# The division of a linear attention: two 32x32-square transposes on VectorE in place of TensorE transposes there and back

## The chip, the cores and the metric

The kernel runs on one NeuronCore of a Trainium2 chip. The metric is device time in microseconds (us); lower is better. The core's engines each take their instructions in order: TensorE (PE; its weight loads are listed apart as PEld), VectorE (DVE), ScalarE (ACT), GpSimd (POOL) and SyncE (SP, which here only starts DMAs). Data lies in SBUF, with 128 partitions; TensorE writes to PSUM, which is used here as 8 banks of 128x512 f32.

## What is computed

One decoder layer over x of shape (32, 128, 256), 32 sequences of 128 positions with 256 features. Three residual blocks, each ahead of a layer norm. Cut to what matters here:

```python
def attn(x):                                  # A: causal linear attention, 16 heads of 16
    q, k = phi(x @ Wq.T + bq), phi(x @ Wk.T + bk)      # phi = elu + 1
    v = x @ Wv.T + bv
    num = einsum('bhsd,bhsde->bhse', q, cumsum(k[..., :, None] * v[..., None, :], 2))
    den = einsum('bhsd,bhsd->bhs', q, cumsum(k, 2))
    return (num / (den[..., None] + 1e-6)) @ Wo.T + bo
x = x + attn(layernorm(x))
x = x + softmax_cross_attention(layernorm(x), ctx_1024)   # B: 16 heads, no output projection
x = x + ffn(layernorm(x))                     # 256 -> 1024 gated, two 1024x1024 gelu layers, -> 256
```

## The kernel before

The 32 sequences are handled as 16 pairs. `xs[m]` holds pair m, 128 positions on the partitions. The first stretch of the program does attention A and attention B, the rest the feed-forward network in eight blocks of four sequences.

**A, for pair m and sequence j of it.** `a_norm` takes statistics on VectorE, finds 1/sqrt on GpSimd by three Newton rounds (lines 145 to 149, twelve tiny instructions), and normalizes on GpSimd. `a_transpose` turns the result to features-on-partitions (TensorE, line 349, and a ScalarE copy). `a_keys` and `a_queries` project it (line 359), apply phi (two Exp and two Relu on ScalarE, lines 463 and 465, then one VectorE instruction, line 467), and for the queries GpSimd makes two copies masked by parity of head (`qa2`, line 381). `a_values` adds the bias to v on VectorE (line 480); next to each head's 16 columns of v stand 16 columns of ones. `a_scores` multiplies keys by queries (line 388, tile `sa`, two halves of two banks each) and VectorE multiplies each half by the causal mask (line 494, tile `at`). `a_weighted` multiplies v with ones by these weights: `pf` has, for head 4i+g, on partitions 32g to 32g+31 and in column block i, 16 rows of the numerator and 16 equal rows of the denominator. It ends with a ScalarE copy to SBUF (`fa`, line 412). `a_divide` transposes the four blocks back on TensorE (`po`, line 419), so that positions lie on the partitions, and VectorE adds the epsilon, takes the reciprocal and multiplies (lines 423, 424, 428). `a_turn` transposes the quotient on TensorE once more (two blocks, `pot`, line 512), and ScalarE copies it to SBUF (`oT`, line 514). `a_out` multiplies by Wo (line 367, `pw`) and VectorE adds to x (line 519).

**B** is softmax attention with the same tiling: `b_maxima` (`sm`, and two VectorE maxima, line 565, 1.2 us each), `b_turn_maxima` (`pz`, `mT`), `b_scores` (`se`, Exp on ScalarE, line 598), `b_weighted` and `b_divide`, which share the functions `weighted` and `divided` with A; b_divide's GpSimd addition is line 606.

**Order.** Every engine's order is the order in which the instructions are written, by lists of units: `first` for steps m = 0, 1, 2; `both` for m = 3 to 15, where A of pair m is interleaved with B of pair m - 3; `begins` for m = 16; then lists with B and feed-forward work only. A unit `(f, ahead, j)` stands for f on pair m + ahead (for b_ units m - 3 + ahead); one that was already done is left out. Before step 0 a short opening does keys, values and queries of the first pairs, after twelve transposes of the identity into a tile that nobody reads (`idle`, line 700).

**Buffers that make one unit wait for another.** The score tiles `sm`, `sa` and `se` share the same four PSUM banks (two tags with one buffer each): `sa` can't be written before VectorE has read `sm`, `se` not before VectorE has read `sa`, the next `sm` not before ScalarE has read `se`. All else on TensorE goes through four other banks (tag `m`). `fa`, `oa`, `oT` have two buffers each.

Of the kernel before, what the change touches and what calls it, by code (L numbers as in the profile page):

```python
# [9 lines left out]
F32 = mybir.dt.float32  # L10
# [3 lines left out]
ALU = mybir.AluOpType  # L14
# [3 lines left out]
P = 128  # L18
B, S, D = 32, 128, 256
H, HD = 16, 16  # L20
HID = 1024
DC = D // P
# [7 lines left out]
VW = 2 * HD  # L30
LN_EPS = 1e-5
ATTN_EPS = 1e-6
# [14 lines left out]
def decoder_block_kernel(  # L47
# [14 lines left out]
    nc = tc.nc  # L62
# [4 lines left out]
    small = ctx.enter_context(tc.tile_pool(name="small", bufs=4))  # L67
# [5 lines left out]
    ident = const.tile([P, P], F32, name="ident")  # L73
# [55 lines left out]
    def pair_stats(n, nmean, rstd, engine=nc.gpsimd):  # L129

        mv = small.tile([P, 2, 2], F32, tag="mv", name="mv")
        for j in range(2):
            st = small.tile([P, 6], F32, tag="st", name="st")
            nc.vector.bn_stats(out=st, in_=xs[n][:, j, :])
            nc.vector.bn_aggr(out=mv[:, j, :], in_=st)
        nc.vector.tensor_scalar(nmean, mv[:, :, 0], -1.0, None, ALU.mult)


        v = small.tile([P, 2], F32, tag="v", name="v")
        nc.vector.tensor_scalar(v, mv[:, :, 1], LN_EPS, None, ALU.add)  # L140
        nc.vector.tensor_scalar(rstd.bitcast(I32), v.bitcast(I32), -0.5, RSQRT_SEED, ALU.mult, ALU.add)
        hv = small.tile([P, 2], F32, tag="hv", name="hv")
        nc.vector.tensor_scalar(hv, v, -0.5, None, ALU.mult)  # L143
        t = small.tile([P, 2], F32, tag="t", name="t")
        for _ in range(NEWTON):
            engine.tensor_tensor(t, rstd, rstd, ALU.mult)  # L146
            engine.tensor_tensor(t, t, hv, ALU.mult)
            engine.tensor_scalar(t, t, 1.5, None, ALU.add)
            engine.tensor_tensor(rstd, rstd, t, ALU.mult)
# [112 lines left out]
    with tc.manual_schedule(engines=ORDERED):  # L262
# [7 lines left out]
        def buffer(shape, dtype, tag, name, **kw):  # L270
            side = att_a if tag in A_TAGS else att_b
            return side.tile(shape, dtype, tag=tag, name=name, **kw)
# [55 lines left out]
        def bank(name):  # L328
            return ps_m.tile([P, 4, S], F32, tag="m", name=name)
# [63 lines left out]
                    stop=stop,  # L393
                )

        def weighted(weights, v, tag):

            pf = bank("pf")
            for i in range(4):
                for g in range(G):
                    nc.tensor.matmul(  # L404
                        pf[32 * g : 32 * g + 32, i, :],
                        lhsT=v[:, 4 * i + g, :],
                        rhs=weights[g // 2][:, g % 2, i, :],
                        start=True,
                        stop=True,
                    )  # L410
            f = buffer([P, 4, S], F32, tag=tag, name=tag)
            nc.scalar.copy(f, pf)
            return f

        def divided(f, add, tag):

            po = bank("po")
            for i in range(4):
                nc.tensor.transpose(po[:, i, :], f[:, i, :], ident)  # L419
            po = po.rearrange("p i (g w) -> p (i g) w", w=VW)  # L420
            rden = small.tile([P, H], F32, tag="rden", name="rden", bufs=2)
            if add:
                nc.vector.tensor_scalar(rden, po[:, :, HD], add, None, ALU.add)
                nc.vector.reciprocal(rden, rden)
            else:
                nc.vector.reciprocal(rden, po[:, :, HD])
            o = buffer([P, D], F32, tag=tag, name=tag)
            nc.vector.tensor_tensor(
                o.rearrange("p (h e) -> p h e", e=HD),
                po[:, :, 0:HD],  # L430
                rden.unsqueeze(2).to_broadcast([P, H, HD]),
                ALU.mult,
            )
            return o
# [8 lines left out]
        A = [dict() for _ in range(NPAIR)]  # L443
# [56 lines left out]
                weights.append(at)  # L500

        def a_weighted(m, j):
            A[m]["f", j] = weighted(A[m].pop(("w", j)), A[m]["v"][:, j], "fa")

        def a_divide(m, j):
            A[m]["o", j] = divided(A[m].pop(("f", j)), ATTN_EPS, "oa")

        def a_turn(m, j):
            pt = bank("pot").rearrange("p a s -> p (a s)")[:, : DC * S]
            o = A[m].pop(("o", j))  # L510
            for c in range(DC):
                nc.tensor.transpose(pt[:, ts(c, P)], o[:, ts(c, P)], ident)
            oT = buffer([P, DC, S], F32, tag="oT", name="oT")
            nc.scalar.copy(oT.rearrange("p c s -> p (c s)"), pt)
            A[m]["oT", j] = oT

        def a_out(m, j):
            pp = token_major(bank("pw").rearrange("p a s -> p (a s)")[:, :D], WO, A[m].pop(("oT", j)))
# [3 lines left out]
        Bs = [dict() for _ in range(NPAIR)]  # L522
# [76 lines left out]
                weights.append(pr)  # L599

        def b_weighted(m, j):
            Bs[m]["f", j] = weighted(Bs[m].pop(("w", j)), Bs[m]["v"][:, j], "fb")

        def b_divide(m, j):
            o = divided(Bs[m].pop(("f", j)), None, "ob")
            nc.gpsimd.tensor_tensor(xs[m][:, j, :], xs[m][:, j, :], o, ALU.add)
            if j == 1:
                pair_stats(m, nmean3[:, 2 * m : 2 * m + 2], rstd3[:, 2 * m : 2 * m + 2])
# [3 lines left out]

        both = [
            (b_maxima, 0, 0), (b_weighted, -1, 1), (a_divide, -1, 1), (b_transpose, 1), (b_values, 1),
            (a_scores, 0, 0), (b_turn_maxima, 0, 0), (b_divide, -1, 1), (a_turn, -1, 1), (a_transpose, 1),
            (b_queries, 1), (b_scores, 0, 0), (a_weighted, 0, 0), (a_out, -1, 1), (b_norm, 2), (a_keys, 1),
            (b_maxima, 0, 1), (b_weighted, 0, 0), (a_divide, 0, 0), (a_bias, 1), (a_queries, 1),
            (a_scores, 0, 1), (b_turn_maxima, 0, 1), (b_divide, 0, 0), (a_turn, 0, 0), (b_keys, 1),
            (b_scores, 0, 1), (a_weighted, 0, 1), (a_out, 0, 0), (a_norm, 2), (a_values, 1), (b_load, 2),
        ]  # L620
        first = [
            (a_scores, 0, 0), (a_norm, 2), (a_turn, -1, 1), (a_keys, 1), (a_out, -1, 1), (b_norm, 2),
            (a_weighted, 0, 0), (a_bias, 0), (a_scores, 0, 1), (a_divide, 0, 0), (a_queries, 1),
            (b_transpose, 1), (a_values, 1), (a_weighted, 0, 1), (a_turn, 0, 0), (a_bias, 1),
            (b_queries, 1), (a_transpose, 2), (a_out, 0, 0), (a_divide, 0, 1), (b_load, 2),
        ]
        prologue = SKEW

# [9 lines left out]
        def settle():  # L638
# [6 lines left out]

        begins = [
            (b_load, 2), (b_maxima, 0, 0), (b_weighted, -1, 1), (a_divide, -1, 1), (b_transpose, 1),
            (b_values, 1), (b_turn_maxima, 0, 0), (a_turn, -1, 1), (b_divide, -1, 1), (a_out, -1, 1), beside,
            (b_queries, 1), (b_scores, 0, 0), beside,
            (b_norm, 2), (b_maxima, 0, 1), settle, (b_weighted, 0, 0), beside,  # L650
            (b_turn_maxima, 0, 1), (b_divide, 0, 0), settle, (b_keys, 1), (b_scores, 0, 1), beside,
# [44 lines left out]
            fill(v)  # L696

        idle = bank("idle")
        for n in range(12):
            nc.tensor.transpose(idle[:, n % 4, :], ident, ident)  # L700
        a_norm(0)
        b_keys(0)
# [10 lines left out]
        for m in range(NPAIR + SKEW + 1):  # L713
            waiting = None
            if m >= prologue and spare:
                n = spare.pop(0)
# [101 lines left out]
    with tc.If(n_inexact > 0):  # L818
        with tc.tile_pool(name="wg", bufs=1) as wg, tc.tile_pool(name="hig", bufs=2) as hig, tc.tile_pool(
            name="ps_g", bufs=8, space=PSUM  # L820
# [23 lines left out]
            for b in range(B):  # L844
# [5 lines left out]
                for c in range(DC):  # L850
                    pt = ps_g.tile([P, TB], F32, tag="mm", name="gpt")
# [90 lines left out]
```

## Time and profile before

| | |
|---|---|
| median of 3 runs | 1135.28 us (1133.74 to 1136.63) |
| profiled execution | 1138.04 us, of which span 1136.2 us |
| attention steps 0 to 2 (list `first`) | 18.8 to 66.4 us of the span |
| attention steps 3 to 15 (list `both`) | 66.4 to 408 us |
| one step of `both` | 28.6 us |
| busy in a step of `both` | PE 28.6, DVE 22.4, ACT 14.0, POOL 17.0 us |
| granted TensorE clock, mean | 0.997 |

The span is what the hardware profiler recorded from the first to the last instruction. A timeline line gives start, duration, engine, source line, operation, output<-inputs, shape and count, and in brackets how long the engine had been idle before it and what ended the wait. Consecutive TensorE instructions overlap, so their durations do not add up: what a group costs TensorE is the distance from its start to the start of the next group.

### The profile page before, as it was taken

What the parts mean: (1) busy time and instruction counts of PE and PEld (TensorE: products, weight loads), DVE (VectorE), ACT (ScalarE), POOL (GpSimd) and SP (SyncE); (2) the same over time, 40 slices, a digit from 0 to 9 for tenths busy, and PEclk for the clock granted to TensorE, in tenths of its full rate; (3) what the DMA queues carried; (4) which work ended last, traced back from release to release, by engine and by line L of the source; (5) the groups of instructions that cost most, each with busy time, mean ns of one, the idle gap of its engine ahead of it and who ended that gap; (6) DMA issues with size and microseconds to landing.
All of it is one profiled execution on the core that took longest, in us unless ns stands there. A gap on an engine that the chain in (4) does not pass through costs nothing.

```text
span 1136.2 us, 20345 instructions
## 1 busy us (share of the span) xinstructions
PE 1117.1 (98%) x8238; PEld 902.7 (79%) x8238; DVE 577.3 (51%) x1296; ACT 411.4 (36%) x655; POOL 446.8 (39%) x1025
## 2 busy tenths in 40 slices
PE   8899999999999999999999999999999999999997
PEld 6677777777777777767888888888888888888886
DVE  6667777777777776532243433522522522422411
ACT  4344444444444446861221221321311312312311
POOL 3655555555555546454231321321311312312311
PEclk9999999999999999999999999999999999999999
DMA  8001111111111100005000111000000000000000
GB/s 274 1 20 48 47 48 48 48 48 48 48 48 48 48 11 11 1 1 185 20 26 31 38 38 38 19 14 5 29 5 5 19 1 2 18 1 15 5 1 22
DMA packets 26548, 39.28 MB, mean 35 GB/s; under 512 B 2512, under 2 KB 18640, under 8 KB 26448
## 3 DMA queue, kind: packets, MB, share of 16 engines
q1 hardware_dynamic: 22000, 26.09, 6.8%
q0 software_dynamic: 4032, 11.54, 3.2%
q8 instruction: 67, 1.10, 0.4%
q10 hardware_dynamic: 416, 0.28, 0.1%
q14 instruction: 33, 0.27, 0.1%
HBM read 33.71 MB, written 4.19 MB: 33 GB/s over the span
## 4 chain that ended last, share of the span: by engine, by line
PE 88%; DVE 3%; POOL 3%; ACT 2%; issue 2%; DMA 1%; SPq 0%; POOLq 0%; DVEq 0%; ACTq 0%
PE ph L218 47%; PE pp L359 9%; PE py L762 5%; PE pf L404 5%; PE pv L367 4%; PE se L388 3%; PE sa L388 3%; PE sm L388 3%; PE pw L367 3%; PE po L419 2%; PE pt L349 1%; DMA H<-in_h2T_dram 1%; DVE at L494 1%; PE se L588 1%; DVE nm L565 1%
## 5 line engine op out<-in xcount | busy, mean ns | idle before, releaser
L181 DVE TENSOR_TENSOR gl<-hg,gh 128x512 fp32r<-128x512 f32 x126 | 87.7, 696 | 345.5 <-POOL gh L180 342.6
L180 POOL CAST gh<-hg 128x512 fp32r<-128x512 f32 x128 | 79.1, 618 | 362.0 <-ACT hg L242 362.0
L242 ACT ACTIVATE hg<-ph,col 128x512 f32<-128x512 f32 x128 | 88.3, 690 | 366.8 <-PE ph L218 366.8
L218 PE MATMUL ph<-sl,H 128*128 128x512 f32 x512 | 199.3, 389 | 0.8 <-POOL sl L181 0.8
L218 PE MATMUL ph<-gl,H 128*128 128x512 f32 x512 | 199.4, 389 | 0.4 <-DVE gl L181 0.4
L218 PE MATMUL ph<-sh,H 128*128 128x512 f32 x512 | 199.6, 390 | 0.1
L218 PE MATMUL ph<-gh,H 128*128 128x512 f32 x512 | 199.4, 390 | 0.0
L218 PEld LDWEIGHTS ph<-sl,H 128*128 128x128 f32 x512 | 96.1, 188 | 21.0 <-POOL sl L181 1.2
L218 PEld LDWEIGHTS ph<-gl,H 128*128 128x128 f32 x512 | 96.1, 188 | 21.0 <-DVE gl L181 1.1
L218 PEld LDWEIGHTS ph<-sh,H 128*128 128x128 f32 x512 | 96.1, 188 | 20.9 <-POOL sh L180 0.6
L218 PEld LDWEIGHTS ph<-gh,H 128*128 128x128 f32 x512 | 96.1, 188 | 20.4 <-POOL gh L180 0.6
L218 PE MATMUL ph<-xh,W 128*128 128x512 f32 x256 | 100.6, 393 | 0.0
L218 PE MATMUL ph<-xl,W 128*128 128x512 f32 x256 | 99.8, 390 | 0.0
L180 POOL CAST sh<-hs 128x512 fp32r<-128x512 f32 x64 | 58.5, 915 | 66.8 <-DVE hs L234 66.8
L565 DVE TENSOR_REDUCE nm<-sm 128x8 f32<-128x1024 f32 x64 | 75.2, 1217 | 17.6 <-PE sm L388 17.6
L494 DVE TENSOR_TENSOR at<-sa,causal 128x1024 f32<-128x1024 f32 x64 | 75.2, 1215 | 8.0 <-PE sa L388 8.0
L232 ACT ACTIVATE sil<-ph,col 128x512 f32<-128x512 f32 x64 | 44.1, 689 | 74.9 <-PE ph L218 74.8
L234 DVE SCALAR_TENSOR_TENSOR hs<-ph,col,sil 128x512 f32<-128x512 f32 x64 | 48.0, 750 | 36.2 <-PE ph L218 20.1
L598 ACT ACTIVATE pr<-se 128x1024 f32<-128x1024 f32 x64 | 62.0, 1022 | 11.9 <-PE se L588 11.9
L146 POOL TENSOR_TENSOR t<-rstd 128x2 f32<-128x2 f32 x138 | 32.5, 235 | 83.3 <-DVE hv L143 76.1
L359 PE MATMUL pp<-xTa,WA 128*128 128x256 f32 x256 | 62.2, 388 | 0.7 <-ACT xTa L351 0.7
L762 PE MATMUL py<-W,gh 128*128 128x256 f32 x256 | 62.6, 285 | 0.0
(133 smaller groups left out, 1933.3 us busy)
## 6 DMA issues: line engine op xcount, KB each, us to landing
x<-in_x_dram SPq DMA_DIRECT2D x16, 256.0 KB, 5.7
cT<-in_ctxT_dram SPq DMA_DIRECT2D x16, 256.0 KB, 2.6
stage<-in_h1T_dram SPq DMA_DIRECT2D x16, 256.0 KB, 2.8
H<-in_h1T_dram POOLq DMA_DIRECT2D x8, 512.0 KB, 3.6
H<-in_h2T_dram POOLq DMA_DIRECT2D x8, 512.0 KB, 8.1
out_dram<-y SPq DMA_DIRECT2D x32, 128.0 KB, 1.7
raw<-in_h2T_dram SPq DMA_DIRECT2D x16, 256.0 KB, 2.8
WA<-in_wattn_dram SPq DMA_DIRECT2D x4, 256.0 KB, 4.7
```

What stands on the lines that cost most here:

```text
L180: (high_engine.copy if high_engine is nc.scalar else high_engine.tensor_copy)(high, t)
L181: lows.append(lambda: low_engine.tensor_tensor(low, t, high.bitcast(F32), ALU.subtract))
L218: nc.tensor.matmul(pp, lhsT=w[:, k, ts(c, P)], rhs=parts[p], start=(k == 0 and p == 0), stop=(k == len(src) - 1 and p == 1),)
L242: nc.scalar.activation(t, pp, AF.Gelu, scale=col[:, c_scale + c : c_scale + c + 1])
L359: nc.tensor.matmul(pp[:, c, :], lhsT=w[:, d, ts(c, P)], rhs=src[:, d, :], start=(d == 0), stop=(d == DC - 1))
L367: nc.tensor.matmul(pp, lhsT=src[:, d, :], rhs=w[:, d, :], start=(d == 0), stop=(d == DC - 1))
L388: nc.tensor.matmul(sc[g // 2][:, g % 2, 2 * c : 2 * c + 2, :], lhsT=loaded[32 * g : 32 * g + 32, c, ts(j, S)], rhs=streamed[32 * g : 32 * ...
L404: nc.tensor.matmul(pf[32 * g : 32 * g + 32, i, :], lhsT=v[:, 4 * i + g, :], rhs=weights[g // 2][:, g % 2, i, :], start=True, stop=True,)
L494: nc.vector.tensor_tensor(at.rearrange("p g i s -> p (g i) s"), sc[u].rearrange("p g i s -> p (g i) s"), causal.unsqueeze(1).to_broadcast( ...
L565: nc.vector.tensor_reduce(nm[:, 2 * u : 2 * u + 2, :], sc[u], AX.X, ALU.max, negate=True)
L598: nc.scalar.activation(pr, sc[u], AF.Exp)
L762: nc.tensor.matmul(py[:, :D], lhsT=h[k][p][:, ts(j, S)], rhs=W3[:, k, :], start=(k == 0 and p == 0), stop=(k == HC - 1 and p == 1),)
```

## The change

In A only, the quotient is formed without TensorE. `weighted` returns `pf`, still in PSUM. `block_divided`, called from `a_weighted`, has VectorE transpose each 32x32 square of `pf` on its own, from PSUM to SBUF: partition 32g+w, block i, position s goes to partition 32g + (s mod 32), block i, square s div 32, column w. Numerator and denominator of a head and position then lie on one partition. VectorE adds the epsilon and takes the reciprocal (now from SBUF), and GpSimd multiplies. `features`, called from `a_divide`, transposes the quotient's squares back on VectorE, which gives features on partitions, in the order of heads that the squares leave. The host permutes the columns of Wo to this order. `a_turn` is gone. B keeps the old way.

With it the lists change: `a_turn` is taken out of `both`, `begins` and `first`; in `first` the units `a_divide` and `b_norm` also stand in other places. The opening's unread transposes go from 12 to 20.

```diff
-            f = buffer([P, 4, S], F32, tag=tag, name=tag)
-            nc.scalar.copy(f, pf)
-            return f
+            return pf
+        def block_divided(pf, add, tags):
+            f = buffer([P, 4, S], F32, tag=tags[0], name=tags[0])
+            nc.vector.transpose(f.rearrange("p i s -> p (i s)"), pf.rearrange("p i s -> p (i s)"))
+            f = f.rearrange("p i (b w) -> p b i w", w=VW)
+            rden = small.tile([P, 4, 4], F32, tag="rden", name="rden", bufs=2)
+            if add:
+                nc.vector.tensor_scalar(rden, f[:, :, :, HD], add, None, ALU.add)
+                nc.vector.reciprocal(rden, rden)
+            else:
+                nc.vector.reciprocal(rden, f[:, :, :, HD])
+            o = buffer([P, 4, 4, HD], F32, tag=tags[1], name=tags[1])
+            nc.gpsimd.tensor_tensor(
+                o, f[:, :, :, 0:HD], rden.unsqueeze(3).to_broadcast([P, 4, 4, HD]), ALU.mult
+            )
+            return o
+        def features(o, tag):
+            oT = buffer([P, DC, S], F32, tag=tag, name=tag)
+            nc.vector.transpose(
+                oT.rearrange("p c (b q) -> p b c q", q=32), o.rearrange("p b (c e) d -> p b c (e d)", e=2)
+            )
+            return oT
...
         def a_weighted(m, j):
-            A[m]["f", j] = weighted(A[m].pop(("w", j)), A[m]["v"][:, j], "fa")
+            pf = weighted(A[m].pop(("w", j)), A[m]["v"][:, j])
+            A[m]["o", j] = block_divided(pf, ATTN_EPS, ("fa", "oa"))
         def a_divide(m, j):
-            A[m]["o", j] = divided(A[m].pop(("f", j)), ATTN_EPS, "oa")
-
-        def a_turn(m, j):
-            pt = bank("pot").rearrange("p a s -> p (a s)")[:, : DC * S]
-            o = A[m].pop(("o", j))
-            for c in range(DC):
-                nc.tensor.transpose(pt[:, ts(c, P)], o[:, ts(c, P)], ident)
-            oT = buffer([P, DC, S], F32, tag="oT", name="oT")
-            nc.scalar.copy(oT.rearrange("p c s -> p (c s)"), pt)
-            A[m]["oT", j] = oT
+            A[m]["oT", j] = features(A[m].pop(("o", j)), "oT")
...
         first = [
-            (a_scores, 0, 0), (a_norm, 2), (a_turn, -1, 1), (a_keys, 1), (a_out, -1, 1), (b_norm, 2),
-            (a_weighted, 0, 0), (a_bias, 0), (a_scores, 0, 1), (a_divide, 0, 0), (a_queries, 1),
-            (b_transpose, 1), (a_values, 1), (a_weighted, 0, 1), (a_turn, 0, 0), (a_bias, 1),
-            (b_queries, 1), (a_transpose, 2), (a_out, 0, 0), (a_divide, 0, 1), (b_load, 2),
+            (a_scores, 0, 0), (a_norm, 2), (a_keys, 1), (a_divide, -1, 1), (a_out, -1, 1),
+            (a_weighted, 0, 0), (a_bias, 0), (a_scores, 0, 1), (a_queries, 1), (a_divide, 0, 0),
+            (b_transpose, 1), (a_values, 1), (a_weighted, 0, 1), (a_bias, 1), (b_norm, 2),
+            (b_queries, 1), (a_transpose, 2), (a_out, 0, 0), (b_load, 2),
         ]
...
         idle = bank("idle")
-        for n in range(12):
+        for n in range(20):
             nc.tensor.transpose(idle[:, n % 4, :], ident, ident)
...
-                (a[n][by_group] if n[-2:] in ("Wq", "Wk") else a[n]).T
+                (a[n][by_group] if n[-2:] in ("Wq", "Wk") else a[n][:, by_group] if n[-2:] == "Wo" else a[n]).T
```

More of the change, by code (lines that the diff above doesn't have):

```diff
@@ L394, in scores, with weighted @@
                 )
-        def weighted(weights, v, tag):
+        def weighted(weights, v):
             pf = bank("pf")
@@ L410, in weighted, with divided @@
                     )
-            f = buffer([P, 4, S], F32, tag=tag, name=tag)
-            nc.scalar.copy(f, pf)
-            return f
-        def divided(f, add, tag):
+            return pf
[20 more added lines that the diff above has]
+            return oT
+        def divided(f, tag):
             po = bank("po")
@@ L421, in divided @@
             rden = small.tile([P, H], F32, tag="rden", name="rden", bufs=2)
[L422 to L426, printed above, removed]
+            nc.vector.reciprocal(rden, po[:, :, HD])
             o = buffer([P, D], F32, tag=tag, name=tag)
@@ L601, in b_weighted @@
         def b_weighted(m, j):
-            Bs[m]["f", j] = weighted(Bs[m].pop(("w", j)), Bs[m]["v"][:, j], "fb")
+            pf = weighted(Bs[m].pop(("w", j)), Bs[m]["v"][:, j])
+            Bs[m]["f", j] = f = buffer([P, 4, S], F32, tag="fb", name="fb")
+            nc.scalar.copy(f, pf)
         def b_divide(m, j):
-            o = divided(Bs[m].pop(("f", j)), None, "ob")
+            o = divided(Bs[m].pop(("f", j)), "ob")
             nc.gpsimd.tensor_tensor(xs[m][:, j, :], xs[m][:, j, :], o, ALU.add)
@@ L614, in decoder_block_kernel @@
             (b_maxima, 0, 0), (b_weighted, -1, 1), (a_divide, -1, 1), (b_transpose, 1), (b_values, 1),
-            (a_scores, 0, 0), (b_turn_maxima, 0, 0), (b_divide, -1, 1), (a_turn, -1, 1), (a_transpose, 1),
+            (a_scores, 0, 0), (b_turn_maxima, 0, 0), (b_divide, -1, 1), (a_transpose, 1),
             (b_queries, 1), (b_scores, 0, 0), (a_weighted, 0, 0), (a_out, -1, 1), (b_norm, 2), (a_keys, 1),
             (b_maxima, 0, 1), (b_weighted, 0, 0), (a_divide, 0, 0), (a_bias, 1), (a_queries, 1),
-            (a_scores, 0, 1), (b_turn_maxima, 0, 1), (b_divide, 0, 0), (a_turn, 0, 0), (b_keys, 1),
+            (a_scores, 0, 1), (b_turn_maxima, 0, 1), (b_divide, 0, 0), (b_keys, 1),
             (b_scores, 0, 1), (a_weighted, 0, 1), (a_out, 0, 0), (a_norm, 2), (a_values, 1), (b_load, 2),
@@ L647, in decoder_block_kernel @@
             (b_load, 2), (b_maxima, 0, 0), (b_weighted, -1, 1), (a_divide, -1, 1), (b_transpose, 1),
-            (b_values, 1), (b_turn_maxima, 0, 0), (a_turn, -1, 1), (b_divide, -1, 1), (a_out, -1, 1), beside,
+            (b_values, 1), (b_turn_maxima, 0, 0), (b_divide, -1, 1), (a_out, -1, 1), beside,
             (b_queries, 1), (b_scores, 0, 0), beside,
```

## The prediction

> **What bounds it now.** I read the page's busy line first, then a table by stage, then TensorE's timeline of one step.
>
> ```profile
> PE 1117.1 (98%) x8238; PEld 902.7 (79%) x8238; DVE 577.3 (51%) x1296; ACT 411.4 (36%) x655; POOL 446.8 (39%) x1025
> ```
>
> ```profile
> 179.10:207.70 28.60, 28.58 (x321) 21.81 (x320) 22.37 (x59) 13.96 (x25) 17.04 (x49) 1.00 0.15 48
> ```
>
> In one step of `both` (columns: length; then busy time of PE, PEld, DVE, ACT, POOL; clock) TensorE has no idle time and VectorE is busy 22.4 of 28.6 us. TensorE work that is taken out shortens the step, unless VectorE, which gets work, is late with something TensorE needs. Where it is close to that shows in the timeline of the step from 207.69 to 236.3:
>
> ```profile
> 209.78 0.66 PE L419 MATMUL po<-ident,fa 128*128 128x128 f32 x4
> 210.27 0.60 PE L349 MATMUL pt<-ident,xnb 128*128 128x128 f32 x4
> ...
> 214.21 0.38 PE L512 MATMUL pot<-ident,oa 128*128 128x128 f32 x2
> 214.43 0.60 PE L349 MATMUL pt<-ident,xna 128*128 128x128 f32 x4
> 215.05 1.99 PE L359 MATMUL pp<-xTb,WB 128*128 128x256 f32 x8
> ...
> 226.49 1.50 PE L388 MATMUL sa<-qa,ka 32*128 32x256 f32 x16
> ...
> 230.56 1.57 PE L388 MATMUL se<-qb,kb 32*128 32x256 f32 x14
> ```
>
> Distances between starts: the four `po` transposes cost 0.49 us, the two `pot` 0.22. An undisturbed score group takes 1.15 us on a line of its own; the `sa` with 1.50 and the `se` with 1.57 already wait inside for the VectorE reads that free their banks.
>
> **What is removed.** Per step two times (0.49 + 0.22) = 1.42 us of TensorE. The `pp` after `pot` and `pt` started 0.62 after `pt` instead of 0.43: it waited for the copy that frees `pot`'s bank, so 0.19 more. At most 1.6 us a step. Two ScalarE copies (0.59 and 0.37 us) go too, worth nothing: ScalarE idles half the step.
>
> **What VectorE gets.** No row shows a square transpose. The nearest rows, one pass over the same shapes:
>
> ```profile
> L480 DVE TENSOR_TENSOR va<-pv,row 128x512 f32<-128x512 f32 x14 | 9.6, 684 | 1.3 <-PE pv L367 1.3
> L428 DVE TENSOR_TENSOR oa<-po,rden 128x256 f32<-128x256 f32 x30 | 12.7, 425 | 1.0
> ```
>
> I take 0.68 us for 128x512 and 0.42 for 128x256 (0.60 and 0.35 start to start). Lower end: the same. Upper end: line 494's 1024 columns take 1215 ns, 0.53 us more than 512, so about 1 ns a column; at twice that the two transposes would take 1.2 and 0.7. A rule speaks against the change: the Trainium skill, "VectorE: DVE Perf Modes", The three transpose paths, gives 311 ns for 128x128 bf16 squares on VectorE. If the cost went with the number of calls of 128 columns, 512 would be 1.24; if a fixed part is paid once, 0.71. The row decides for the latter, the former is my upper end. Addition and reciprocal stay (0.17 + 0.25), the 0.42 multiply leaves VectorE. Balance: +0.68 per sequence, 1.4 a step: 23.7 of some 27.2 us.
>
> **Where it lies.** (1) The 128x512 transpose comes behind `pf`, ahead of the x addition. There VectorE now waits:
>
> ```profile
> 206.07 0.42 DVE L519 TENSOR_TENSOR x<-pw,x 128x256 f32<-128x256 f32 x1 [2.31 <-PE pw L367]
> ...
> 220.47 0.42 DVE L519 TENSOR_TENSOR x<-pw,x 128x256 f32<-128x256 f32 x1 [1.14 <-PE pw L367]
> ```
>
> `pf` was done at 204.97; transpose, addition and reciprocal end at 204.97 + 0.6 + 0.2 + 0.3 = 206.1: hidden to within 0.1. Every further 0.1 us of transpose comes out late. What is then late: statistics, v, the weight tests, the maxima (line 565) and so `sa`. (2) The 128x256 transpose (0.35) takes the place of 0.9 us of division between maxima and mask; VectorE gets there 0.5 us sooner.
>
> Walking the step (time from its start; before in brackets): maxima end 4.55 (4.5); TensorE reaches `sa` at 4.35 (4.84) and half of it waits: end 5.6 (5.9). `se` at 8.4 (9.3), its `pot` and the bank wait gone. `pf` 9.7, keys end 13.5 (14.4), then Exp/Relu, line 467 and maxima to 18.2 (19.1). TensorE, without the second `po`, is at the second `sa` at 17.4 and waits to 18.2: this `po`'s 0.49 is half lost here. Masks end 22.05 (23.4), because the short transpose replaced the division; second `se` and `pf` follow 1.3 us sooner. **The step is 27.3 us, 1.3 less.** Twelve such, and 0.9 in step 3: -16.5. Step 16: -0.6.
>
> **GpSimd gets** a multiply of 128x256 with two inputs, like line 606 (0.72 us; the broadcast and the rows of 16 are in no row: 0.5 to 1.5). That is 1.45 a step beside 17.0. In the step it is hidden: the first multiply ends about 16.7 and is wanted at 18.6, the second has over 5 us; only above 2.7 us would it make the short transpose late, and with it the masks. In the opening it isn't hidden.
>
> **The opening, steps 0 to 2.** Here waits set the time:
>
> ```profile
> 48.85 1.15 PE L388 MATMUL sa<-qa,ka 32*128 32x256 f32 x16 [2.79 <-POOL qa L381]
> 49.92 0.44 PE L512 MATMUL pot<-ident,oa 128*128 128x128 f32 x2
> 50.20 3.54 PE L359 MATMUL pp<-xTa,WA 128*128 128x256 f32 x8
> ```
>
> ```profile
> 50.00:60.00 10.00, 10.00 (x82) 0.83 0.00 1
> ```
>
> After 2.8 us of idling the clock fell (0.83 here, i.e. 3.4 us at half): eight matmuls took 3.33 us instead of 1.73, 1.6 lost. In the new list `b_norm` (Newton and normalize, 4.8 us of GpSimd) no longer stands ahead of the queries' masks: that wait goes. But others come. Step 0: GpSimd is the chain (Newton, normalize, bias, masks) and has one multiply more: +0.7. Steps 1 and 2: `a_out` of the pair before stands behind `a_divide`, whose VectorE transpose is queued behind masks, statistics and line 467. `pw` can start some 6.1 and 7.3 us into the step, where TensorE is free at 2.8: idling 3.4 and 4.5 us, then `pf`, the next scores and their masks are late. Step 1 still gets 1.7 shorter, as the masks are sooner; step 2 0.8 longer. Sum of the three: -0.2. Step 3: `b_norm(1)` now comes after the last `a_weighted` of step 2, and `b_transpose(1)` is the second thing TensorE does in step 3. From the end of `pf`: transpose, addition and reciprocal 1.1, then on GpSimd multiply 0.72 and bias 1.4 (the statistics, 1.7, lie beside these), Newton and normalize 4.8: 8.0 us; TensorE has 1.7 + 0.4 + 0.9 + 1.1 = 4.1 to do. It waits 4 us. And each of these four idle stretches can drop the clock, 1.6 us each: I take two net of the one that goes, +3.5 (0 to 5).
>
> The eight extra idle transposes:
>
> ```profile
> 1.47 2.82 PE L700 MATMUL idle<-ident 128*128 128x128 f32 x12 [1.47 <-POOL ident masks.py:199]
> 5.67 3.75 PE L359 MATMUL pp<-cT,WB 128*128 128x256 f32 x8 [1.38 <-DMA cT<-in_ctxT_dram]
> ```
>
> The first eight real matmuls take 3.75 us, as in the slow stretch above: the array starts slow. Twenty at the same 0.22 us fill the gap to 5.9. If they make it fast sooner, up to 1.5 us are won, before the first layer norm limits; if transposes don't count as work, as "TensorE: Matmul & The Clock Gate", PE-mode transpose, has it, they only delay by 0.3. The trace decides nothing: twelve weren't enough. I take -0.8.
>
> Opening: -0.2 + 4 + 3.5 - 0.8 = +6.5 (2 to 10).
>
> **Sum.** -16.5 - 0.6 + 6.5 = -10.6. The profiled execution took 1138.04 us, span 1136.2 and 1.84 around it, 2.8 above the median; taken from the median, 1135.28 - 10.6 = **1124.7 us**.
>
> **Rivals.** *Opening costs nothing* (0.17): no clock drops, the unread transposes help, waits are covered; then -17 to -20: 1115 to 1119. For it: the masks' wait goes. Against: the order of VectorE's queue. *VectorE becomes the bound, gain eaten up* (0.13): transposes at the upper end, 0.54 more. Step gain 1.3 - 0.54 = 0.76, and in the opening about five transposes lie on the path, +2.7: -10.6 + 7.0 + 2.7 = -0.9, 1134.4, no change. *Slower* (0.2): the square transpose costs three cycles an element, 1.75 us, 1.07 more; -10.6 + 18 x 1.07 = +8.7, 1144. It decides from -10.6 + 18 d = 0, d = 0.59, i.e. 1.27 us for 128x512. For it: no row of such a transpose, and the place at which it lies has 0.1 us of cover. Against: all VectorE rows of this size lie at 0.68 to 0.75 whatever the operation.
>
> **Chances and range.** Forecast 0.5 (own range 1119 to 1131), rivals 0.17, 0.13, 0.2. A time within 0.3% (3.4 us) of the median can't be told from no change. Faster: 0.5 + 0.17 + 0.03 = 0.7; same 0.1; slower 0.2. Leaving out little below and about half of the slower case: 1114 to 1140.
>
> **What would show it.** Steps of `both` at 27.3 us; a 128x512 transpose at 0.68 and the x addition not later than 0.1 us after `pw`; `sa` waiting on line 565; waits of `pw` on the short transpose in steps 1 and 2, and of `pt` on `xnb` in step 3. The forecast is wrong if the transpose is longer than 1 us, if TensorE waits elsewhere in `both`, or if steps 0 to 2 end well before 66 us.

## The result

The changed kernel takes 1133.69 us (median of 20 runs, 1131.58 to 1135.55) against 1136.12 for the kernel before (20 runs, 1133.74 to 1138.48): ratio 0.9976, 95% interval 0.9969 to 0.9983. It is 2.4 us faster where 10.6 were forecast; the range of 1114 to 1140 holds it, the size of the gain was wrong. The interval lies below 1, but the gain is less than the 0.3% (3.4 us) that the prediction took as the least that can be told from no change. The profiled execution took 1133.88 us, span 1132.0. Against the profiled execution of the kernel before, whose span was 1136.2, that is 4.2 us; this is the difference that the stages below add up to. It is larger than the 2.4 of the medians: the profiled execution of the kernel before was 1.9 us above its median, and its step 2 holds 1.8 us of slow clock that another profile of the same instructions does not have (first experiment). Two runs far from all others, 1236.7 us of the doubled transpose (granted clock 0.84) and 2803.6 of the kernel before, are left out of medians and ratios.

The step that was to bring the gain did bring it. The page's busy line of the changed kernel, and its table for one step of `both` (length; busy PE, PEld, DVE, ACT, POOL; clock):

```profile
PE 1100.5 (97%) x8054; PEld 887.7 (78%) x8054; DVE 599.7 (53%) x1328; ACT 382.8 (34%) x591; POOL 467.7 (41%) x1057
```

```profile
211.48:238.93 27.45, 27.05 (x307) 20.59 (x306) 23.76 (x60) 12.15 (x21) 18.35 (x51) 1.00 0.15 50
```

28.62 us became 27.45. VectorE is at 23.8 (23.7 was the prediction's sum). TensorE's timeline of that step shows the same places as before:

```profile
213.57 0.65 PE L349 MATMUL pt<-ident,xnb 128*128 128x128 f32 x4
214.06 1.89 PE L367 MATMUL pv<-WB,cT 128*128 128x256 f32 x8
215.89 1.33 PE L388 MATMUL sa<-qa,ka 32*128 32x256 f32 x16
...
229.12 0.70 PE L388 MATMUL sa<-qa,ka 32*128 32x256 f32 x4
230.22 1.13 PE L388 MATMUL sa<-qa,ka 32*128 32x256 f32 x12 [0.40 <-DVE nm L579]
```

`po` and `pot` of the linear attention are gone, and both `sa` now wait inside for the maxima: the second is cut in two by an idle 0.4 us. The new operations, by the groups from 100 to 400 us, which is steps 4 to 14 (shape, count, busy us and mean ns of one):

```profile
L419 DVE STREAM_TRANSPOSE fa<-pf 128x512 f32<-128x512 f32 x21 | 15.0, 713 | 12.8 <-PE pf L404 12.8
L436 DVE STREAM_TRANSPOSE oT<-oa 128x256 f32<-128x256 f32 x22 | 9.6, 435 | 0.0
...
L489 DVE SCALAR_TENSOR_TENSOR ka<-e,r 128x512 f32<-128x512 f32 x11 | 11.4, 1034 | 12.2 <-ACT r L487 12.2
```

The square transposes take 0.71 and 0.44 us, as taken from the rows of before (0.68, 0.42). The keys' instruction, line 489 here and 467 before, went from 0.69 to 1.03 us although nothing in it changed. Before (30 to 430 us):

```profile
L467 DVE SCALAR_TENSOR_TENSOR ka<-e,r 128x512 f32<-128x512 f32 x14 | 9.7, 694 | 17.3 <-ACT r L465 17.3
```

Where the rest went shows when the program is cut at the first score group of each step (starts in TensorE's timelines; length in us). Before the change the list `both` runs to 431.5 us: the 408 us of the table of times before is where step 15, its last step, begins.

| | before | changed | difference | predicted |
|---|---|---|---|---|
| start to step 0 | 18.78 | 17.36 | -1.4 | -0.8 |
| step 0 | 13.48 | 14.00 | +0.5 | +0.7 |
| step 1 | 16.59 | 18.41 | +1.8 | -1.7, and clock |
| step 2 | 17.55 | 21.02 | +3.5 | +0.8, and clock |
| step 3 | 26.82 | 30.88 | +4.1 | -0.9 + 4, and clock |
| steps 4 to 14 | 314.8 | 302.0 | -12.8 | -14.3 |
| step 15 | 23.51 | 26.29 | +2.8 | -1.3 |
| step 16 to the end | 704.7 | 702.1 | -2.6 | -0.6 |
| sum | 1136.2 | 1132.0 | -4.2 | -10.6 |

The predicted price of the clock is 3.5 us over steps 1 to 3, which is in the sum. So three parts of the sum matter: steps 1 to 3 lost 9.3 us (+5.7 predicted), step 15 lost 2.8, and an ordinary step won 1.17 instead of 1.3. The waits and the clock behind them, in TensorE's timeline of the changed kernel:

```profile
37.62 2.05 PE L367 MATMUL pw<-WA,oT 128*128 128x256 f32 x4 [3.18 <-DVE oT L436]
39.59 1.94 PE L404 MATMUL pf<-at,va 128*32 128x128 f32 x32
41.46 2.09 PE L388 MATMUL sa<-qa,ka 32*128 32x256 f32 x16
...
57.91 2.04 PE L367 MATMUL pw<-WA,oT 128*128 128x256 f32 x4 [5.07 <-DVE oT L436]
...
75.15 1.23 PE L349 MATMUL pt<-ident,xnb 128*128 128x128 f32 x4 [3.22 <-POOL xnb L339]
76.18 2.80 PE L367 MATMUL pv<-WB,cT 128*128 128x256 f32 x8
...
419.08 3.21 PE L388 MATMUL sa<-qa,ka 32*128 32x256 f32 x16 [1.91 <-DVE nm L579]
...
423.33 3.30 PE L359 MATMUL pp<-cT,WB 128*128 128x256 f32 x8
```

After each idle stretch the groups take up to twice their usual time (`sa` 2.09 instead of 1.15, eight projections 3.30 instead of 1.89; the 3.21 of the last `sa` also holds a wait for the second maxima). The granted clock fell with them (columns: length, PE busy, clock):

```profile
30.00:50.00 20.00, 15.73 (x138) 0.83 0.00 1
410.00:430.00 20.00, 17.96 (x199) 0.83 0.05 14
```

From 50 to 60, 60 to 72 and 72 to 90 us it is 0.88, 0.96 and 0.91. Before, it was 1.00 in all these stretches but for the 0.83 from 50 to 60. The first three waits are the ones that the prediction named; the fourth it had not looked for. The first is for the short transpose, which stands behind the statistics and line 489 in VectorE's queue:

```profile
34.82 0.42 DVE L134 BATCH_NORM_STATS2 st<-x 128x6 f32<-128x256 f32 x1
...
36.43 0.69 DVE L489 SCALAR_TENSOR_TENSOR ka<-e,r 128x512 f32<-128x512 f32 x1
37.03 0.44 DVE L436 STREAM_TRANSPOSE oT<-oa 128x256 f32<-128x256 f32 x1
```

The fourth lies in step 15, where TensorE waited before the change too, but less:

```profile
423.31 0.70 PE L388 MATMUL sa<-qa,ka 32*128 32x256 f32 x4 [0.55 <-DVE nm L565]
424.43 1.13 PE L388 MATMUL sa<-qa,ka 32*128 32x256 f32 x12 [0.43 <-DVE nm L565]
```

### The profile page after: what moved, and what is told of

The parts are those of the page before. It is cut to its first block, busy times and chain, and to the rows that moved or that the text cites. A ratio compares the mean times of both kernels' runs of the same rounds, so it can differ in the third digit from the quotient of the medians.

```text
span 1132.0 us, 19943 instructions
## 1 busy us (share of the span) xinstructions
PE 1100.5 (97%) x8054; PEld 887.7 (78%) x8054; DVE 599.7 (53%) x1328; ACT 382.8 (34%) x591; POOL 467.7 (41%) x1057
## 4 chain that ended last, share of the span: by engine, by line
PE 78%; DVE 12%; ACT 4%; POOL 4%; issue 2%; POOLq 0%; DVEq 0%; ACTq 0%
PE ph L218 50%; PE py L778 5%; PE pv L367 4%; PE pp L359 4%; DVE at L516 3%; PE sa L388 3%; DVE nm L579 3%; PE pf L404 3%; PE se L388 2%; PE pw L367 2%; PE sm L388 2%; DVE ka L489 1%; ACT e L485 1%; ACT r L487 1%; PE pt L349 1%
## 5 line engine op out<-in xcount | busy, mean ns | idle before, releaser
L778 PE MATMUL py<-W,gl 128*128 128x256 f32 x256 | 62.0, 283 | 0.0
```

Of the source, the lines that this page charges most:

```text
L778: nc.tensor.matmul(py[:, :D], lhsT=h[k][p][:, ts(j, S)], rhs=W3[:, k, :], start=(k == 0 and p == 0), stop=(k == HC - 1 and p == 1),)
```

## The experiments

The theory: the gain of the steps is real, and the order of the units gives most of it back, through waits at which the clock falls as well. The rivals: VectorE has too much work wherever the transposes lie; the transposes or GpSimd's multiply cost more than their own time. Each ratio is to the kernel before, run in turn on the same chip. Differences to the changed kernel in us are between medians taken at different times, in part on different chips; the intervals of the ratios (1 to 4 us on either side) hold for them at the least.

**The unread transposes alone, in the kernel before.**

```diff
-        for n in range(12):
+        for n in range(20):
```

> The kernel before with only the opening's unread transposes raised from 12 to 20. If transposes count as work for the clock, the first eight projections (3.75 us before) take about 2.2 us as in the changed kernel, the first score group starts at 17.4 instead of 18.8 us, and the time falls by about 1.4 us (ratio 0.9988). If they do not count (the page on the clock gate), the start is at the same slow pace and 0 to 0.3 us later.

Measured 1135.4 us, ratio 0.9987 (0.9978 to 0.9995). The timeline of the start:

```profile
1.46 4.37 PE L700 MATMUL idle<-ident 128*128 128x128 f32 x20 [1.46 <-POOL ident masks.py:199]
6.02 1.97 PE L359 MATMUL pp<-cT,WB 128*128 128x256 f32 x8 [0.19 <-DMA cT<-in_ctxT_dram]
```

The first eight projections take 1.97 us instead of 3.75 and step 0 begins at 17.53 instead of 18.78. Transposes of the identity do make the array fast. The Trainium skill ("TensorE: Matmul & The Clock Gate", PE-mode transpose) has it that the full clock does not engage for transposes; here the measurement decides. It rests on the durations, since the granted clock reads 1.00 over the first 16 us in both kernels. About 1.3 us of the changed kernel's gain is this, and has nothing to do with the division.

The same run shows that a wait need not bring the clock down. In step 2 TensorE has the wait for the masks that the kernel before has (2.79 us there), and the projections behind it are not slow (3.54 us there):

```profile
47.59 1.15 PE L388 MATMUL sa<-qa,ka 32*128 32x256 f32 x16 [2.80 <-POOL qa L381]
...
48.94 1.89 PE L359 MATMUL pp<-xTa,WA 128*128 128x256 f32 x8
```

Step 2 takes 15.79 us here, 17.55 in the profile of before.

**The short transpose first in steps 0 to 2.**

```diff
-            (a_scores, 0, 0), (a_norm, 2), (a_keys, 1), (a_divide, -1, 1), (a_out, -1, 1),
+            (a_divide, -1, 1), (a_scores, 0, 0), (a_norm, 2), (a_keys, 1), (a_out, -1, 1),
```

> The changed kernel with one unit moved: in the list of steps 0 to 2 the short transpose of the pair before stands first in the step, ahead of the masks, statistics and keys. Theory of the queue: the waits of pw on it (3.2 us in step 1, 5.1 in step 2) and the slow clock behind them go; steps 1 and 2 take 15 to 16 and 17 to 18.5 us instead of 18.4 and 21.0; the time falls by 5 to 8 us, to about 1127. Rival, VectorE simply has too much work there: the wait moves from pw to the next scores' masks, and less than 2 us are won.

Measured 1124.96 us, ratio 0.9898 (0.9880 to 0.9915): 8.7 us less than the changed kernel, from one unit moved, a little more than the 5 to 8 expected. Step 1 takes 12.95 us instead of 18.41, step 2 16.05 instead of 21.02; but step 3 takes 33.55 instead of 30.88, because TensorE gets there sooner and waits 4.6 us for `xnb`. VectorE had time for all its work in steps 1 and 2; what it lacked was the right order.

**And b_transpose later, in all steps from 3 on.**

```diff
-            (b_maxima, 0, 0), (b_weighted, -1, 1), (a_divide, -1, 1), (b_transpose, 1), (b_values, 1),
-            (a_scores, 0, 0), (b_turn_maxima, 0, 0), (b_divide, -1, 1), (a_transpose, 1),
+            (b_maxima, 0, 0), (b_weighted, -1, 1), (a_divide, -1, 1), (b_values, 1),
+            (a_scores, 0, 0), (b_turn_maxima, 0, 0), (b_transpose, 1), (b_divide, -1, 1), (a_transpose, 1),
```

> As the kernel with the short transpose first, and in the steps from 3 on b_transpose moved behind the first linear scores (TensorE has b_values, scores and pz to do before it). Theory: the wait of pt for xnb in step 3 (3.2 us idle and a slow clock after it) falls to about 1 us; 3 to 4 us less than the kernel with the short transpose first, no change in the length of the other steps (27.45). Rival, the normalized x is late for everything in step 3: the wait moves to the next projection and less than 1 us is won.

Measured 1126.01 us, ratio 0.9911 (0.9893 to 0.9929). Step 3 fell to 28.62 us, 4.9 less, but all the other steps rose from 27.45 to 27.96, against the expectation. TensorE now comes to the first `sa` 0.4 us sooner, waits there for the maxima (1.72 us for the group), and does the transposes of `xnb` behind it, where nothing waits. VectorE, not TensorE, says when the first `sa` can be written. So the 0.43 us of transposes were free ahead of it; behind it they cost what they take.

**GpSimd's masks moved, for line 489.**

```diff
             nc.scalar.copy(q, pp)
-            Bs[m]["q2"] = masked(q, C_PARS, "qb2")
+        def b_masks(m):
+            Bs[m]["q2"] = masked(Bs[m]["q"], C_PARS, "qb2")
...
-... (b_norm, 2), (a_keys, 1),
+... (b_norm, 2), (b_masks, 1), (a_keys, 1),
```

In the other lists the new unit stands directly behind `b_queries`.

> The changed kernel with GpSimd's two masks of the cross attention's queries moved behind the layer norm that follows. Theory: line 467's instruction for the keys takes 1.03 us instead of 0.69 because it now runs beside these masks and the new multiply, which read SBUF too; with them moved it takes 0.7 to 0.8, and a step falls from 27.45 to about 27.15 us, 3 to 4 us in all (about 1130.3). Rival, it is long for its own operands or the multiply alone blocks it: it stays at 1.0 and the step at 27.45.

Measured 1133.62 us, ratio 0.9971 (0.9959 to 0.9983): no gain over the changed kernel. But the group did what the theory said:

```profile
L489 DVE SCALAR_TENSOR_TENSOR e<-e,r 128x512 f32<-128x512 f32 x11 | 7.9, 714 | 2.5 <-ACT r L487 2.5
L489 DVE SCALAR_TENSOR_TENSOR ka<-e,r 128x512 f32<-128x512 f32 x11 | 7.6, 694 | 12.2 <-ACT r L487 12.2
```

The keys' instruction is back at 0.69 us, GpSimd's multiply at 0.62 (0.84 in the changed kernel). They block each other when they run side by side; the Trainium skill has such a rule ("SBUF — State Buffer", Who interferes with whom: a VectorE instruction with two SBUF inputs and a GpSimd instruction that reads SBUF), and these numbers fit it. The step stays at 27.47 because the 0.34 us won are waited for one instruction on: the queries' line 489 now idles 0.23 us for ScalarE's Relu. In the changed kernel that Relu, behind TensorE's projection, was just as late (it ends at 230.80, VectorE gets to line 489 at 230.86), hidden by the longer keys.

Step 1 of this profile adds to the clock. `pw` waits as long for the short transpose as in the changed kernel, and nothing behind it is slow:

```profile
37.84 1.10 PE L367 MATMUL pw<-WA,oT 128*128 128x256 f32 x4 [3.19 <-DVE oT L436]
38.88 1.08 PE L404 MATMUL pf<-at,va 128*32 128x128 f32 x32
```

The step takes 15.49 us instead of 18.41; in another run below it takes 16.88, with the same wait and instructions. Whether and for how long the clock falls behind a wait of 3.2 us differs from one execution to the next.

**The clock alone.** TensorE's idle time in the opening is filled with transposes that nobody reads.

```diff
+        def unread(count):
+            idle = bank("idle")
+            for n in range(count):
+                nc.tensor.transpose(idle[:, n % 4, :], ident, ident)
...
         def a_out(m, j):
+            if m < 2 and j == 1:
+                unread((24, 40)[m])
...
         def b_transpose(m):
+            if m == 1:
+                unread(24)
```

> The changed kernel with unread transposes of the identity put on TensorE where it idles in the opening: 24 and 40 ahead of pw in steps 1 and 2, 24 ahead of pt in step 3 (0.11 us each, less than the idle time there). Nothing else moves, so the waits stay and only the clock can change. Theory: the slow clock after the three waits costs by itself; pw, pf and scores in step 1 take 1.1, 1.1, 1.15 us again instead of 2.05, 1.94, 2.09, likewise in steps 2 and 3, and 4 to 6 us are won (about 1128.5). Rival: VectorE and GpSimd set the time in the opening, so a slow TensorE costs nothing: less than 1.5 us.

Measured 1127.92 us, ratio 0.9921 (0.9892 to 0.9950), 5.8 us less than the changed kernel (give or take 3, by the interval), as expected, though what TensorE waits for comes no sooner. The granted clock is 1.00 from 50 to 90 us. Steps 1 to 3 are 16.82, 19.57 and 29.74 us: 1.6, 1.5 and 1.1 less, 4.2 in all; 1.2 more comes from step 15 (25.08 instead of 26.29), whose units were not touched. Step 15 lies between 25.1 and 26.4 us in all changed kernels that leave the statistics there and do each transpose once, so how much the clock takes there differs too. In step 1 the first scores and keys were slow still, after the waits in step 0, for which no filling was put in.

**The long transpose twice.**

```diff
             nc.vector.transpose(f.rearrange("p i s -> p (i s)"), pf.rearrange("p i s -> p (i s)"))
+            nc.vector.transpose(f.rearrange("p i s -> p (i s)"), pf.rearrange("p i s -> p (i s)"))
```

> The changed kernel with every 128x512 square transpose done twice in a row (0.65 us more VectorE work per sequence, same result). By the prediction's walk only the second sequence's transpose has no cover: a step gets 0.6 us longer (27.45 to 28.05), the first sequence's is hidden by the wait ahead of line 467; with some 3 us in the opening about +11 us, 1144. Rival A, VectorE is the bound of the whole step: +1.3 us a step, +20 us in all. Rival B, it has cover left: less than +3 us.

Measured 1149.16 us, ratio 1.0109 (1.0075 to 1.0144), 15.5 us more than the changed kernel; the step takes 28.58 us, 1.13 more, between the expected 0.6 and rival A's 1.3. That is not one extra transpose (0.75 us start to start) but one and a half. VectorE's timeline of the step behind the first sequence's pair:

```profile
231.23 0.72 DVE L420 STREAM_TRANSPOSE fa<-pf 128x512 f32<-128x512 f32 x1
...
233.92 0.61 DVE L140 TENSOR_SCALAR v<-mv 128x2 f32<-128x2 f32 x1
234.57 0.64 DVE L141 TENSOR_SCALAR rstd<-v 128x2 int32<-128x2 int32 x1
...
235.18 1.14 DVE L490 SCALAR_TENSOR_TENSOR ka<-e,r 128x512 f32<-128x512 f32 x1
```

and what GpSimd did meanwhile:

```profile
233.82 1.37 POOL L381 TENSOR_SCALAR qb<-qb,col 128x512 f32<-128x512 f32 x2
235.15 0.62 POOL L429 TENSOR_TENSOR oa<-fa,rden 128x256 f32<-128x256 f32 x1
```

Two statistics instructions on two columns, 0.17 us otherwise, take 0.6 beside the masks. So the first sequence's cover of 1.1 us was used up by the transpose and by what it pushed beside GpSimd.

**The long transpose twice, masks moved.** Both edits above together.

> The 128x512 transpose done twice, and GpSimd's masks of the cross attention's queries moved behind the layer norm. With the transpose done twice alone a step took 28.58 us, 1.13 more. Theory: the first sequence's extra transpose has cover (1.1 us of VectorE idling ahead of line 467), but pushed the small statistics instructions and line 467 beside these masks, where they took 0.61, 0.64 and 1.14 us instead of 0.17, 0.17 and 0.69; with the masks elsewhere they are short again and the step takes about 28.1 us. Rival, the 0.75 us of the first sequence were on the path by themselves: 28.5 or more.

Measured 1146.81 us, ratio 1.0096 (1.0081 to 1.0112); the step takes 28.31 us, above the theory's 28.1 and below the rival's 28.5. Lines 140 and 141 are back at 0.15 and 0.17 us, line 490 at 0.69. In their place line 136 takes 0.58 instead of 0.17, beside the multiply (232.70 to 233.3), which now comes there. Against the 27.47 with masks moved alone that is 0.84 us for 1.5 us of transposes: about one of the two is on the path.

**Multiply on VectorE.** `nc.vector.tensor_tensor` in place of `nc.gpsimd.tensor_tensor` in `block_divided`.

> The changed kernel with the multiply of the quotient on VectorE instead of GpSimd. If GpSimd's share is hidden in the steps, as predicted, and VectorE's second transpose has no cover: 0.35 us a step more (27.45 to 27.8), about +4.5 in steps 3 to 15, less up to 1 us in the opening where GpSimd is the chain: +3.5, 1137. Rival, the GpSimd multiply costs time by blocking VectorE's two-input instructions: the step stays or gets shorter.

Measured 1141.02 us, ratio 1.0033 (1.0016 to 1.0051): 7.3 us more than the changed kernel, twice the 3.5 expected. The step takes 27.97 us, 0.52 more, and the opening and step 3 did not get shorter (step 2 22.96, step 3 31.72). The multiply is cheaper on GpSimd, although it blocks VectorE at times. The keys' line 489 still takes 0.93 us here, beside the masks alone, so the multiply is not needed to lengthen it.

**Statistics later, in step 15 alone.**

```diff
+        fifteenth = [u for u in both if u != (b_norm, 2)]
+        fifteenth.insert(fifteenth.index((b_maxima, 0, 1)) + 1, (b_norm, 2))
...
-                first if m < prologue else both if m < NPAIR
+                first if m < prologue else both if m < NPAIR - 1 else fifteenth if m < NPAIR
```

> The changed kernel with b_norm behind the maxima of the second sequence in step 15 alone (the step without keys and queries of a next pair). Theory: there TensorE waits 1.9 us for the maxima, which now stand behind transpose and statistics, and the clock drops after it (scores 3.2 us, keys 3.3); with 1.65 us of statistics out of the way the step goes from 26.3 to about 23.5 us: 2 to 3 us less. Rival: the wait moves to the next mask and nothing is won.

Measured 1129.99 us, ratio 0.9941 (0.9919 to 0.9963), 3.7 less than the changed kernel. Step 15 takes 23.50 us, 2.8 less, as before the change. Shorter than before it does not get: TensorE now waits 0.30 and 0.43 us for the maxima and 0.51 and 0.43 for the masks behind them. The other 0.9 is outside the step and within the spread: steps 1 to 3 of this profile, ahead of the edit and with the same instructions, are 16.88, 21.74 and 31.32 us instead of 18.41, 21.02 and 30.88, and the stretch from step 16 on is 0.7 shorter.

**The list of steps 0 to 2 as it was before**, with `a_divide` where `a_turn` stood.

```diff
-            (a_scores, 0, 0), (a_norm, 2), (a_keys, 1), (a_divide, -1, 1), (a_out, -1, 1),
-            (a_weighted, 0, 0), (a_bias, 0), (a_scores, 0, 1), (a_queries, 1), (a_divide, 0, 0),
-            (b_transpose, 1), (a_values, 1), (a_weighted, 0, 1), (a_bias, 1), (b_norm, 2),
+            (a_scores, 0, 0), (a_norm, 2), (a_divide, -1, 1), (a_keys, 1), (a_out, -1, 1), (b_norm, 2),
+            (a_weighted, 0, 0), (a_bias, 0), (a_scores, 0, 1), (a_queries, 1),
+            (b_transpose, 1), (a_values, 1), (a_weighted, 0, 1), (a_divide, 0, 0), (a_bias, 1),
```

> The changed kernel with the list of steps 0 to 2 in the order it had before the change, the short transpose where a_turn stood (so b_norm again ahead of the first a_weighted). Theory: the wait of pt in step 3 goes (step 3 at 26.5 to 27 instead of 30.9), the wait for the queries' masks comes back, now with a multiply more ahead of them (3 to 4 us in step 1 or 2), and the short transpose is still behind statistics in VectorE's queue (pw waits about 2 us): steps 1 and 2 at 17 to 19 us each, 3 to 6 us less than the changed kernel, about 1129. Rival, the new list is what the new order of work needs: the old one is slower than it.

Measured 1124.51 us, ratio 0.9898 (0.9878 to 0.9918), 9.2 less than the changed kernel, 4 to 5 us better than expected. Steps 1 to 3 take 18.14, 17.44 and 26.14 us: step 3 has no wait for `xnb`, `pw` waits 2.6 us for the short transpose in steps 1 and 2, and the scores of step 2 do not wait for the masks as they did before the change, since `pw` ahead of them waits for its own 1.5 us. Of the two waits of 2.6 us one is followed by slow matmuls (step 1), the other is not. So the new order of this list, one part of the change, cost 9.2 us of the 12.8 that the new division won in steps 4 to 14.

**The three orders together**: short transpose first in steps 0 to 2, `b_transpose` later in step 3 alone, statistics later in step 15 alone.

> The changed kernel with three pieces of order put right: the short transpose first in steps 0 to 2, b_transpose behind the first scores in step 3 alone, b_norm behind the second maxima in step 15 alone. From the runs of the single pieces: steps 1 and 2 at 13 and 16 us, step 3 at 28.6 instead of 33.6, steps 4 to 14 at 27.45, step 15 at 23.5 instead of 25.1: 1125 - 4.9 - 1.6 = about 1118.5. If step 3's gain is given back later, as when b_transpose was moved in every step, 1123.

Measured 1118.84 us, ratio 0.9859 (0.9843 to 0.9875). Steps 1 to 3: 12.91, 16.04, 28.61; 4 to 14: 27.45; 15: 23.50. It is 17.0 us faster than the kernel before on the same chip, and 14.9 below the changed kernel's 1133.69 (13.3 by the ratios).

**With the masks moved too.**

> The three pieces of order together with the masks moved behind the layer norm. Moved alone, the masks gave line 467 its 0.69 us back but the step stayed at 27.47, since the queries' Relu then set the time. Expected: no difference from the kernel with the three pieces of order, within 1 us; if anything else in the step gains, up to 2 us less.

Measured 1119.27 us, ratio 0.9854 (0.9840 to 0.9867): no difference, as expected.

## Why the prediction was wrong, and what in it held

The mechanism of an ordinary step held. Two terms of the sum failed: step 15 was counted among the "twelve such", and the opening with its clock was put too low. Against the profiled difference the sum is off by 6.4 us: 4.1 in step 15, 3.6 in steps 1 to 3, 1.5 in steps 4 to 14, less 2.8 that the start, step 0 and the stretch from step 16 on gave beyond what was predicted.

- **TensorE is the bound, 1.3 us a step**: held in kind, 1.17 in size. The transposes are right to 0.03 us; 0.71 for the long one is also what a fixed part paid once would give, and far from the 1.24 of the upper end. The walk put the second masks (line 494, now 516) at 19.8 us after the step's start; the trace has 231.44 - 211.48 = 19.96, set by the queries' Relu, for which the walk has no time. The longer line 489 is not the cause: with it short again the step stayed. Over eleven steps this is 1.5 us.
- **"Twelve such"**: the step that failed most. It took step 15 for a step like the others. Step 15 has no keys and queries of a next pair for TensorE, so VectorE is its bound. Before the change TensorE already idled there for the maxima, 0.55 and 0.43 us, and I did not look. With transpose, addition and reciprocal ahead of the statistics the wait became 1.9 us and the clock fell: +2.8 instead of -1.3, 4.1 us of the 6.4. The second `sa` starts 15.4 us into the step (15.3 before): the longer wait took what was won ahead of it. From there to the end of the step it is 10.9 us instead of 8.2, with the clock at 0.83. The run with the statistics moved shows the cause of the 2.8; the 1.3 that were forecast do not come there either, since VectorE still bounds the step.
- **The opening**: the three waits came where they were named (3.2 and 5.1 us for `pw`, predicted 3.4 and 4.5; 3.2 us for `pt`, predicted 4). Without any slow clock the walk gives steps 1 to 3 as 16.59 - 1.7, 17.55 + 0.8 and 26.82 + 3.1, 63.2 us. The run with filled idle time has 66.1, of which step 1's first scores and keys (1.78 and 3.01 us instead of 1.15 and 1.99) are still some 1.65 of slow clock: 64.5. So the walk is 1.3 short, and the clock costs about 70.3 - 64.5 = 5.8 us. The prediction had 3.5, "two net of the one that goes". That step failed by counting twice: step 2's "0.8 longer" compares a walk at full clock with a step of before that contains the drop, so the drop that goes was in it already (without it that step takes 15.79 us). The granted clocks of the changed kernel give (0.17 x 20 + 0.12 x 10 + 0.04 x 12 + 0.09 x 18) / 0.5 = 13.4 us at half between 30 and 90 us, four times the 3.4 that the prediction read for one drop: none of the drops in steps 1 to 3 could be taken off. The price of 1.6 us a drop is no fixed one either: behind the same wait in step 1 it was 2.9, 1.4 and 0 us in three profiles, so how near any such sum comes is in part luck.
- **The unread transposes**, taken as -0.8 between -1.5 and +0.3: -1.3 to -1.4.
- **Cover of the long transpose**: "hidden to within 0.1" for what was taken; the doubled transpose shows how little there is beyond. The break-even of 0.59 us more rested on one sequence's transpose in each step; doubled, it cost 15.5 us instead of the 13.5 that 18 x 0.75 gives from the changed kernel, since the first sequence's loses its cover beside GpSimd.
- **Step 16 on**: -2.6, not -0.6. 1.0 of it lies between `pf` and `pw` of step 16 (3.78 us instead of 4.79), where `po`, `pot` and a wait of 0.19 for `oT` are gone. The rest is not traced, and part of it may be spread between executions: the kernel before with 20 unread transposes has 703.5 us for this stretch against the 704.7 of before, with the same instructions in it.
- **The rivals**: none came as it was written. VectorE is not out of time in an ordinary step, and the transpose has the price of any instruction of its shape; only in step 15 is VectorE the bound. That the time lies within 0.7 us of the 1134.4 of "gain eaten up" is chance: that rival rested on a longer transpose.

## What to carry to other kernels

When work moves between engines whose order is written out by hand, cost the first and last rounds of the loop by themselves: they lack the work that covers the move in the middle, and here they gave back nearly all of 12.8 us. Ask of every moved unit what stands ahead of it in the new engine's queue, since a 0.4 us instruction behind some 3 us of mask, statistics and keys stopped TensorE for 3 us here; and count a long idle stretch on TensorE (1.9 us and more here) as possibly longer than it looks: the work after it often ran slower, though not each time, so one profile of such a stretch is not its price.

## What the runs showed of the hardware

A VectorE instruction took 0.34 to 0.47 us longer, even one on two columns (0.61 and 0.64 instead of 0.16 and 0.17), when GpSimd read and wrote large SBUF tiles beside it, and GpSimd's multiply went from 0.62 to 1.05 us in the same stretch. Moving the GpSimd work undid it for these instructions in both experiments; in the second it came back at another one beside the multiply. Transposes count for the clock: twenty of them instead of twelve let the first eight projections take 1.97 us instead of 3.75, and with 24 to 40 in idle stretches the granted clock was 1.00 from 50 to 90 us instead of 0.88 to 0.96. A wait of TensorE does not always bring the clock down: behind a wait of 3.2 us in step 1, with the same instructions, the slow clock cost 2.9, 1.4 and 0 us in three profiles.
